# Softmax running sums: VectorE additions become accumulating transfers in GpSimd's queue

## The chip, the cores and the metric

The kernel runs on one core of a Trainium2 chip. The metric is the device time of one execution in microseconds (us). Beside it stands a profile: one execution recorded by the hardware profiler, with the busy time of each engine, what each waited for, and the transfers.

## The reference

The kernel computes a self-attention block on a feature map `x` of shape (16, 512, 32, 32) in float32: 16 images, 512 channels, 1024 positions, 4 heads of 128 channels each.

```python
xn = group_norm(x, 8 groups) * gamma + beta
q, k, v = split(einsum('oc,bchw->bohw', qkv_w, xn) + qkv_b, 3)   # to heads: (b, 4, 1024, 128)
attn = softmax(einsum('bhnd,bhmd->bhnm', q, k) * 128 ** -0.5)
out = einsum('bhnm,bhmd->bhnd', attn, v)                          # back to (b, 512, 32, 32)
return x + einsum('oc,bchw->bohw', proj_w, out) + proj_b
```

## The kernel before

The work is a sequence of **steps**, one for each image `b`, head `h` and block `j` of 128 keys: 16 x 4 x 8 = 512 steps. Keys lie on the 128 partitions and the 1024 queries along the row. In step `s`:

- `scores(s, half)` (L844 on): TensorE multiplies the key block by 512 queries (L846, tile `s` in PSUM), and ScalarE writes the exponentials into `p` (L852). A `p` tile is 128 x 1024, 512 KB; there are three of them.
- The softmax's denominators are the sums of the exponentials over all keys. VectorE first adds the eight blocks element by element into the tile `tot`: at block 1 it writes `tot` as the sum of blocks 0 and 1 (L858), and at blocks 2 to 7 it adds `p` to `tot` (L860). There is one `tot` tile.
- `weighted_sum(s - 1, half)` (L942): TensorE multiplies the values by the step before's `p`, adding over the eight blocks in the PSUM tile `po`. At the last block ScalarE copies `po` to the tile `o` (L949).

At block 1 of the next head `denominators` (L864 on) finishes the head before: VectorE transposes `tot` in 32 x 32 blocks (L869), reduces it (L871), adds the four partial results, transposes and takes the reciprocal (L879). Two transfers from ScalarE's queue spread it over the partitions (L891, L896, tile `rinv`), and at block 4 VectorE multiplies `o` by it (`divide`, L952). The very last head has its own ending, `last_division`, which lets TensorE do the sums over partitions.

Between the steps' products TensorE does the projections in 256- and 512-wide products by Strassen's scheme on two levels, spread over the heads by `plan_head`: queries and keys of the second head pair in head 0 (tiles `qk_*`), the output projection of the image before in head 1 (`pp_*`), queries and keys of the next image in head 2, its values in head 3 (`v_*`). For each product VectorE makes sums of the right-hand blocks (L574, tiles `qk_t`, `pp_t`), and VectorE and ScalarE empty the accumulators (L630, L486, L628). The weights' sums are kept in DRAM and come group by group by SP's queue into two buffers (`w<-kept`, L408).

GpSimd's queue carries transfers in the kernel before: `x` of the next image (L235), sums of the right-hand blocks that are used again (`kept_t`, L580), the values on their way through DRAM for a change of layout (`vd<-vu`, L779, then four `v<-vd`, L784, which wait for it), the residual `y<-in_x` (L813) and the result (L830). The tiles `vt`, `vu` and most `y` share four buffers with the tag "y".

A scheduler orders each engine's instructions when the kernel is built, by priority and by the order in which the program states them; each engine then runs its list in that order and waits on semaphores. `tc.high_priority(URGENT)` raises a priority, and `tc.issue_after(ins)` keeps the instructions inside it behind the named one. The dictionary `added` holds the additions to `tot` for that purpose: the group norm's small steps for the next image (`stats_group`), the first right-hand sums of the next image (`make_sum`), and `divide` are placed after the addition of a given block.

Of the kernel before, what the change touches and what calls it, by code (L numbers as in the profile page):

```python
# [13 lines left out]
ALU = mybir.AluOpType  # L14
# [13 lines left out]
URGENT = 40  # L28
# [158 lines left out]
def fast_path(ctx, tc, x, sources, out, consts, flag, dims):  # L187
# [6 lines left out]
    nc = tc.nc  # L194
    B, C, N, NCC, NH2, NB, GC, SCALE = dims
# [76 lines left out]
    def stats_group(b):  # L272


        g = []

        def part(n, first, last):
            if not g:
                g.extend(norm.group_steps(mvs[b]))
            with tc.issue_after(added[b - 1, 1, n].ins), tc.high_priority(URGENT):  # L280
                for step in g[first:last]:
                    step()

        def scale():
            n = 4 if b > 1 else 3
            part(n, 9, 10)
            with tc.issue_after(added[b - 1, 1, n].ins), tc.high_priority(URGENT):
                mu, sc = norm.result
                sh = norm.shift(mu, sc)
            for c in range(NCC):  # L290
                scaled[b, c] = sc, sh, c

        return [lambda: part(2, 0, 6), lambda: part(3, 6, 9), scale]
# [174 lines left out]
    def run(units):  # L468
        for u in units:
            u()  # L470
# [52 lines left out]
    def two_levels(name, site, b, blocks, finish, sums="make", homes="BBBB", prepare=None):  # L523
# [18 lines left out]
        def sum_tile(g, m):  # L542
            k = int(m[1]) - 1
            tag = f"in_{m}" if homes[g] == "B" else f"ot{2 + k // 2}{k % 2}"
            if homes[g] == "C":
                if k % 2 == 0:
                    pairs[g] = ppool.tile([P, N], F32, tag="p", name=f"{name}_{g}_{m}")
                t = pairs[g][:, ts(k % 2, HALF)]
            else:
                t = tpool.tile([P, HALF], F32, tag=tag, name=f"{name}_{g}_{m}")  # L550
            haves[g][m] = t.rearrange("p (i q) -> p i q", q=Q)
            return haves[g][m][:, : len(OUTER[g])]

        def inner_block(g, i, m):
            if m[0] == "t":
                return haves[g][m][:, i, :]
            outer = blocks()[FACTORS[OUTER[g][i]][1]]
            return outer[int(m[1]) - 1][:, ts(int(m[2]) - 1, Q)]

        def make_sum(g, m):  # L560
            n = len(OUTER[g])
            to = sum_tile(g, m)
            a, c = {
                "t1": ("b12", "b11"), "t2": ("b22", "t1"), "t3": ("t2", "b11"),
                "t4": ("b21", "t2"),
            }[m]
            with ExitStack() as order:
                if sums == "keep" and g == 0 and m in ("t1", "t2"):


                    order.enter_context(tc.issue_after(added[b - 1, 1, NB - 1].ins))
                    order.enter_context(tc.high_priority(URGENT))
                for i in range(n):
                    nc.vector.tensor_sub(  # L574
                        to[:, i, :], inner_block(g, i, a), inner_block(g, i, c)
                    )
            if sums == "keep":
                t = dpool.tile([P, n, Q], F32, tag=f"{m}_{g}", bufs=1, name=f"kept_{m}_{g}")
                inner_kept[b, g, m] = t
                nc.gpsimd.dma_start(t, to)  # L580
# [125 lines left out]
    def qk_groups(b, pair):  # L706

        def finish(which, r, a, c):
            of, half = int(which[1]) - 1, int(which[2]) - 1
            st, h = (qs, ks)[of], 2 * pair + r  # L710
            if (b, h) not in st:
                st[b, h] = qkpool.tile([P, N], F32, tag=f"qk{of}", name=f"qk{of}_{b}_{h}")
            i = of * HEADS + h
            nc.vector.scalar_tensor_tensor(  # L714
                st[b, h][:, ts(half, HALF)], a, qkb_sb[:, i : i + 1], c, ALU.add, ALU.add
            )

        return two_levels(
            f"qk_{b}_{pair}", pair, b, lambda: xb[b], finish,
            "make" if pair or b == 0 else "keep",  # L720
            "ABBB" if pair else "ABAB" if b > 0 else "BCBC",
        )
# [33 lines left out]
    def v_groups(b):  # L756
        rows = {}


        def finish(which, h, a, c):  # L760
            pair, half = int(which[1]) - 1, int(which[2]) - 1
            if (b, pair) not in vs:
                vs[b, pair] = vpool.tile(
                    [P, NH2, 2, P, NB // NH2], F32, tag="v", name=f"v_{b}_{pair}"
                )
            n = P // BLK
            t = ypool.tile([P, HALF], F32, tag="y", name=f"vt_{b}_{pair}_{h}_{half}")
            nc.vector.tensor_add(t, a, c)

            u = ypool.tile([P, HALF], F32, tag="y", name=f"vu_{b}_{pair}_{h}_{half}")  # L770
            nc.vector.transpose(  # L771
                u.rearrange("p (q i j) -> p j q i", q=n, i=BLK),
                t.rearrange("p (j q i) -> p j q i", q=n, i=BLK),
            )
            if h == 0:
                rows[which] = dpool.tile(
                    [2 * P, HALF], F32, tag="v", name=f"vd_{b}_{pair}_{half}"
                )
            nc.gpsimd.dma_start(rows[which][ts(h, P), :], u)  # L779
            if h == 0:  # L780
                return

            for q in range(n):
                nc.gpsimd.dma_start(  # L784
                    vs[b, pair][ts(q, BLK), half].rearrange(
                        "m h (k i) j -> m (h k) (i j)", k=n
                    ),
                    rows[which].rearrange("(k m) (q e) -> q m k e", m=BLK, q=n)[q],
                )

        return two_levels(f"v_{b}", "v", b, lambda: xb[b], finish, "load", "ABAB")
# [43 lines left out]
    ps, tot, po, rinv, last_eviction = {}, {}, {}, {}, {}  # L835
    inverse, rows_of, added, exps = {}, {}, {}, {}
    steps = B * HEADS * NB

    def where(s):
        bh, j = divmod(s, NB)  # L840
        return (*divmod(bh, HEADS), j)

    def scores(s, half):
        b, h, j = where(s)  # L844
        sc = ps_s.tile([P, HALF], F32, tag="s", name=f"s_{s}_{half}")
        nc.tensor.matmul(  # L846
            sc, ks[b, h][:, ts(j, P)], qs[b, h][:, ts(half, HALF)], start=True, stop=True
        )
        if half == 0:
            ps[s] = ppool.tile([P, N], F32, tag="p", name=f"p_{s}")  # L850
        with tc.high_priority(URGENT):
            exps[s] = nc.scalar.activation(ps[s][:, ts(half, HALF)], sc, AF.Exp, scale=SCALE)  # L852
        i = ts(half, HALF) if s == steps - 1 else ds(0, N)
        if j == 0 or (half == 0 and s < steps - 1):
            return
        if j == 1:
            tot[b, h] = lpool.tile([P, N], F32, tag="tot", name=f"tot_{b}_{h}")
            nc.vector.tensor_add(tot[b, h], ps[s - 1], ps[s])  # L858
        else:
            added[b, h, j] = nc.vector.tensor_add(  # L860
                tot[b, h][:, i], tot[b, h][:, i], ps[s][:, i]
            )

    def denominators(b, h):  # L864

# [85 lines left out]
    def divide(b, h):  # L951
        nc.vector.tensor_mul(os_[b, h], os_[b, h], rinv.pop((b, h)))  # L952
# [288 lines left out]
    for s in range(steps + 1):  # L1241
        units = []
        if s < steps:
            b, h, j = where(s)
            if j == 0:
                plan = plan_head(b, h)
            units = plan[j]
            if j == NB - 1 and h == 2 and b + 1 < B:
                next_v.append(v_groups(b + 1))
                next_qk.append(qk_groups(b + 1, 1))  # L1250
                units.append(ahead[f"v_{b + 1}"])
        if NB < s < steps and s % NB == 1:
            denominators(*where(s - 2)[:2])
        for half in range(NH2):
            if s < steps:
                scores(s, half)
                if j in (1, 2) and half == 1 and s > NB:
                    with tc.issue_after(exps[s].ins):
                        spread_inverse(*where(s - NB)[:2], j - 1)
                if half == 1 and j == 4 and s > NB:  # L1260

                    with tc.issue_after(added[b, h, 4].ins):
                        divide(*where(s - NB)[:2])
            if s > 0:
                weighted_sum(s - 1, half)
            n = (len(units) + 1) // 2
            run(units[half * n : (half + 1) * n])
        if s > 0:
            del ps[s - 1]
# [134 lines left out]
```

## Time and profile before

| what | value |
|---|---|
| time, median of 2 runs | 3171.86 us (3171.75 to 3171.98) |
| the profiled execution's span | 3170.7 us |
| granted TensorE clock | 1.000 |
| TensorE busy | 3159.9 us (100%) |
| VectorE busy | 2633.6 us (83%) |
| ScalarE busy | 1439.7 us (45%) |
| GpSimd busy | 517.7 us (16%) |
| additions L860 | 385, 1218 ns each, 469.0 us in all |
| transfers | 524.32 MB, mean 165 GB/s |

The span runs from the first to the last instruction that the profiler recorded; the time of a run also holds what lies around it. A line of the cost table names the program line, the engine, the operation, the written and the read tiles, the shapes and the count, then the busy time, the mean of one, and the idle time ahead of them with what ended most of it. A line of the transfers names the issuing queue, the count, the size of each and the median time from issue to landing. The timeline's columns are start, duration, engine, line, operation and, in brackets, the idle time ahead of it and what ended it.

### The profile page before, as it was taken

How to read it: one execution, taken by the hardware profiler on the slowest of the kernel's cores; microseconds unless marked ns; L12 is line 12 of the kernel's file. 1: busy time of each engine (PE TensorE's matmuls, PEld its weight loads, DVE VectorE, ACT ScalarE, POOL GpSimd, SP SyncE). 2: the span in 40 equal slices, each digit the busy share in tenths (PEclk: the TensorE clock that was granted, in tenths of full speed). 3: DMA queues.
4: the chain of work that ended last, by engine and by line, in shares of the span. 5: the costliest groups of instructions: out<-in, count | busy, mean ns of one | idle time of the engine just before them, and what ended most of it. 6: DMA issues, size and time to landing. Idle time of an engine off the chain costs nothing.

```text
span 3170.7 us, 34267 instructions
## 1 busy us (share of the span) xinstructions
PE 3159.9 (100%) x10524; PEld 2190.7 (69%) x10524; DVE 2633.6 (83%) x4639; ACT 1439.7 (45%) x2712; POOL 517.7 (16%) x898
## 2 busy tenths in 40 slices
PE   9999999999999999999999999999999999999999
PEld 7566676677766676777767767677676776766764
DVE  9878879788897888878788787987879978788784
ACT  3535435354353543545435453453534545344342
POOL 0011221111211112211122111222012221122200
PEclk9999999999999999999999999999999999999999
DMA  5554554555545455454554545555455564555531
GB/s 177 185 190 154 188 172 154 171 153 192 171 164 162 153 185 175 167 167 145 191 172 162 171 145 187 171 172 172 144 175 169 176 189 134 174 162 186 179 116 41
DMA packets 210333, 524.32 MB, mean 165 GB/s; under 512 B 32096, under 2 KB 65376, under 8 KB 210144
## 3 DMA queue, kind: packets, MB, share of 16 engines
q1 hardware_dynamic: 132896, 282.12, 28.8%
q0 software_dynamic: 64000, 204.54, 19.2%
q10 hardware_dynamic: 13248, 35.39, 3.5%
q8 instruction: 87, 1.43, 0.2%
q14 instruction: 102, 0.84, 0.1%
HBM read 388.77 MB, written 133.17 MB: 165 GB/s over the span
## 4 chain that ended last, share of the span: by engine, by line
PE 96%; DVE 3%; DMA 0%; issue 0%; POOL 0%; SPq 0%; ACT 0%; DVEq 0%; POOLq 0%
PE po L942 27%; PE s L846 27%; PE qk_x L606 12%; PE qk_y L606 9%; PE pp_x L606 6%; PE v_x L606 6%; PE pp_y L606 4%; PE v_y L606 4%; PE lx L1031 0%; DVE qk_t L574 0%; PE ly L1031 0%; PE warm L1153 0%; DVE tot L860 0%; DVE qk L714 0%; DVE qk_r L630 0%
## 5 line engine op out<-in xcount | busy, mean ns | idle before, releaser
L942 PE MATMUL po<-p,v 128*128 128x512 f32 x2048 | 1049.5, 594 | 0.7 <-ACT p L852 0.7
L846 PE MATMUL s<-qk,qk 128*128 128x512 f32 x2048 | 1047.4, 593 | 0.3 <-DVE qk L714 0.3
L852 ACT ACTIVATE p<-s 128x512 f32<-128x512 f32 x1024 | 610.9, 597 | 961.0 <-PE s L846 957.2
L942 PEld LDWEIGHTS po<-p,v 128*128 128x128 f32 x2048 | 603.6, 302 | 322.7 <-issue 214.5
L860 DVE TENSOR_TENSOR tot<-tot,p 128x1024 f32<-128x1024 f32 x385 | 469.0, 1218 | 158.4 <-ACT p L852 156.3
L846 PEld LDWEIGHTS s<-qk,qk 128*128 128x128 f32 x2048 | 387.7, 190 | 88.6 <-issue 29.9
L606 PEld LDWEIGHTS qk_x<-qk_t,w 128*128 128x128 f32 x1344 | 251.8, 190 | 166.1 <-issue 75.3
L606 PE MATMUL qk_x<-qk_t,w 128*128 128x256 f32 x1344 | 356.3, 382 | 0.1
L486 ACT COPY qk_u<-qk_x 128x512 f32<-128x512 f32 (+1 forms) x256 | 136.3, 533 | 229.2 <-PE qk_x L606 229.2
L779 POOL DMA_DIRECT2D vd<-vu x120 | 66.7, 557 | 899.8 <-DVE vu L771 897.9
L630 DVE TENSOR_TENSOR qk_r<-qk_y,qk_u 128x512 f32<-128x512 f32 (+1 forms) x256 | 157.7, 616 | 34.7 <-ACT qk_u L486 21.6
L580 POOL DMA_DIRECT2D kept_t<-qk_t x240 | 129.4, 540 | 278.4 <-DVE qk_t L574 211.9
L606 PEld LDWEIGHTS pp_x<-pp_t,w_proj 128*128 128x128 f32 x630 | 117.2, 190 | 74.7 <-issue 32.3
L784 POOL DMA_DIRECT2D v<-vd x240 | 140.6, 593 | 167.1 <-DMA vd<-vu 70.3
L630 DVE TENSOR_TENSOR v_r<-v_y,v_u 128x512 f32<-128x512 f32 (+1 forms) x120 | 76.0, 633 | 110.6 <-ACT v_u L486 80.3
L606 PE MATMUL pp_x<-pp_t,w_proj 128*128 128x256 f32 x630 | 167.8, 383 | 0.0
L606 PE MATMUL v_x<-v_t,w_v 128*128 128x256 f32 x630 | 166.6, 381 | 0.0
L830 POOL DMA_DIRECT2D out_y<-y x120 | 66.0, 550 | 604.2 <-DVE y L829 602.4
L606 PEld LDWEIGHTS v_x<-v_t,w_v 128*128 128x128 f32 x630 | 118.4, 190 | 55.3 <-issue 19.1
L606 PE MATMUL qk_y<-x,w 128*128 128x256 f32 x512 | 142.1, 379 | 0.0
L714 DVE SCALAR_TENSOR_TENSOR qk<-qk_r,qkb_sb,qk_r 128x512 f32<-128x512 f32 x192 | 137.5, 743 | 1.6
L486 ACT COPY v_u<-v_x 128x512 f32<-128x512 f32 (+1 forms) x124 | 66.3, 535 | 157.1 <-PE v_x L606 130.3
(217 smaller groups left out, 4487.2 us busy)
## 6 DMA issues: line engine op xcount, KB each, us to landing
w<-kept SPq DMA_DIRECT2D x90, 512.0 KB, 3.7
kept_t<-qk_t POOLq DMA_DIRECT2D x180, 256.0 KB, 3.3
v_t<-kept_t SPq DMA_DIRECT2D x180, 256.0 KB, 2.9
w<-kept SPq DMA_DIRECT2D x90, 384.0 KB, 3.4
rinv<-row ACTq DMA_DIRECT2D x63, 512.0 KB, 4.9
x<-in_x POOLq DMA_DIRECT2D x60, 512.0 KB, 4.6
vd<-vu POOLq DMA_DIRECT2D x120, 256.0 KB, 3.1
v<-vd POOLq DMA_DIRECT2D x240, 128.0 KB, 4.2
```

The lines of the kernel that those rows point to most:

```text
L486: nc.scalar.copy(t[n][:, :width], t["x"][:, :width])
L580: nc.gpsimd.dma_start(t, to)
L606: nc.tensor.matmul(acc[:, ts(i, Q)], have["w"][t][:, i, slot, :], inner(i, bn), start=(first and i == 0), stop=True, skip_group_check=True,)
L630: nc.vector.tensor_add(dst, view(a), view(c))
L714: nc.vector.scalar_tensor_tensor(st[b, h][:, ts(half, HALF)], a, qkb_sb[:, i : i + 1], c, ALU.add, ALU.add)
L779: nc.gpsimd.dma_start(rows[which][ts(h, P), :], u)
L784: nc.gpsimd.dma_start(vs[b, pair][ts(q, BLK), half].rearrange("m h (k i) j -> m (h k) (i j)", k=n), rows[which].rearrange("(k m) (q e) -> ...
L830: nc.gpsimd.dma_start(out[b, ts(o, P), ts(half, HALF)], t)
L846: nc.tensor.matmul(sc, ks[b, h][:, ts(j, P)], qs[b, h][:, ts(half, HALF)], start=True, stop=True)
L852: exps[s] = nc.scalar.activation(ps[s][:, ts(half, HALF)], sc, AF.Exp, scale=SCALE)
L860: added[b, h, j] = nc.vector.tensor_add(tot[b, h][:, i], tot[b, h][:, i], ps[s][:, i])
L942: nc.tensor.matmul(po[b, h][:, i], v_block(b, h, j), ps[s][:, i], start=(j == 0), stop=(j == NB - 1),)
```

## The change

From block 2 of each head on, the addition of `p` to `tot` is no longer an instruction of VectorE but a transfer in GpSimd's queue whose destination is `tot` and which adds to what is there (`accum_op=ALU.add`). Block 1's addition, which writes `tot` first, stays on VectorE, and so do all additions of the last head of the last image (`s >= steps - NB`). Each transfer reads a whole `p` tile, 512 KB, once both halves of its exponentials are written, and needs the transfer before it to have landed in `tot`; `p` is free again when its transfer has read it and the weighted sum has used it.

Since a transfer isn't an instruction of VectorE, `added` now holds, for these blocks, the last instruction stated so far for VectorE (`last_on_vector`); the places that order work behind `added` are otherwise the same.

```diff
+    def last_on_vector():
+
+        return next(
+            i for i in reversed(nc.cur_bb.bb.instructions) if i.engine == mybir.EngineType.DVE
+        )
...
         if j == 1:
             tot[b, h] = lpool.tile([P, N], F32, tag="tot", name=f"tot_{b}_{h}")
             nc.vector.tensor_add(tot[b, h], ps[s - 1], ps[s])
-        else:
+        elif s >= steps - NB:
             added[b, h, j] = nc.vector.tensor_add(
                 tot[b, h][:, i], tot[b, h][:, i], ps[s][:, i]
-            )
+            ).ins
+        else:
+            nc.gpsimd.dma_start(tot[b, h], ps[s], accum_op=ALU.add)
+            added[b, h, j] = last_on_vector()
...
-            with tc.issue_after(added[b - 1, 1, n].ins), tc.high_priority(URGENT):
+            with tc.issue_after(added[b - 1, 1, n]), tc.high_priority(URGENT):
```

The last pair of lines stands for four places that read `added` (two in `stats_group`, one in `make_sum`, one ahead of `divide`): they lose `.ins`, since `added` now holds the instruction itself.

More of the change, by code (lines that the diff above doesn't have):

```diff
@@ L286, in scale @@
             part(n, 9, 10)
-            with tc.issue_after(added[b - 1, 1, n].ins), tc.high_priority(URGENT):
+            with tc.issue_after(added[b - 1, 1, n]), tc.high_priority(URGENT):
                 mu, sc = norm.result
@@ L568, in make_sum @@
                 if sums == "keep" and g == 0 and m in ("t1", "t2"):
-                    order.enter_context(tc.issue_after(added[b - 1, 1, NB - 1].ins))
+                    order.enter_context(tc.issue_after(added[b - 1, 1, NB - 1]))
                     order.enter_context(tc.high_priority(URGENT))
@@ L1260, in fast_path @@
                 if half == 1 and j == 4 and s > NB:
-                    with tc.issue_after(added[b, h, 4].ins):
+                    with tc.issue_after(added[b, h, 4]):
                         divide(*where(s - NB)[:2])
```

## The prediction

> **What bounds the kernel now.** I read the page's engine line and chain first, then the group of the edited line, then four neighbouring heads as windows, and last the transfers and the waits.
>
> ```profile
> PE 3159.9 (100%) x10524; PEld 2190.7 (69%) x10524; DVE 2633.6 (83%) x4639; ACT 1439.7 (45%) x2712; POOL 517.7 (16%) x898
> PE 96%; DVE 3%; DMA 0%; issue 0%; POOL 0%; SPq 0%; ACT 0%; DVEq 0%; POOLq 0%
> L860 DVE TENSOR_TENSOR tot<-tot,p 128x1024 f32<-128x1024 f32 x385 | 469.0, 1218 | 158.4 <-ACT p L852 156.3
> ```
>
> TensorE is busy all the time, and 96% of the chain that ended last is TensorE. The edited line L860 is VectorE work and isn't in that chain by name. The windows (image 8, one head each; columns are the stretch, its length, then busy time and count of PE, PEld, DVE, ACT, POOL, the granted clock, the DMA share and GB/s) ask whether "busy" hides slack:
>
> ```profile
> 1612.00:1661.00 49.00, 49.00 (x164) 34.51 (x163) 43.48 (x73) 19.05 (x35) 13.55 (x24) 1.00 0.57 176
> 1661.00:1710.00 49.00, 49.00 (x166) 34.11 (x166) 42.09 (x84) 33.60 (x70) 6.18 (x9) 1.00 0.41 137
> 1710.00:1759.00 49.00, 49.00 (x164) 34.47 (x164) 44.31 (x79) 19.05 (x34) 9.69 (x18) 1.00 0.61 207
> 1759.00:1808.00 49.00, 49.00 (x164) 34.43 (x163) 34.36 (x54) 19.21 (x35) 4.55 (x8) 1.00 0.50 152
> ```
>
> A head's 164 matmuls are 64 of 512 columns (s and po, 8 blocks x 2 halves x 2 products x 2 passes) and 100 of 256. Back to back, the timeline spaces the former 0.43 us apart and the latter 0.216 us (eight in 1.73 us on the chain): 64 x 0.43 + 100 x 0.216 = 49.1 us. That is the whole 49.0 us. So a head has no slack on TensorE that a freer VectorE could win. What can be won lies at the two ends and is at most 3170.7 - 3159.9 = 10.8 us by the busy time. The profiled span, 3170.7 us, is 1.2 us under the median of the runs, 3171.86; I add to the latter.
>
> **What is removed.** 63 heads x 6 blocks = 378 of the 385 adds; the last head's 7 stay. 378 x 1.218 = 460 us of VectorE, 7.3 us a head. By the paragraph above this buys nothing on the path: I take 0, bounds 0 to -10.8 us. VectorE falls to some 2170 us, 69%.
>
> **What is added.** 378 transfers of 512 KB in GpSimd's queue, each reading p and the running sum and writing the sum. Each also needs the sum that the one before left, so within a head they form a chain of six. Issue: POOL rows show 0.54 us for a transfer, so 378 x 0.54 = 204 us, and POOL goes from 517.7 to some 720 us, 23%: no bound. The traffic:
>
> ```profile
> q0 software_dynamic: 64000, 204.54, 19.2%
> ```
>
> 378 x 0.524 = 198 MB more in that queue is 18.6% of the sixteen engines if it moves like the copies there, and 37% if each byte costs two. With today's queues (28.8 + 19.2 + 3.5 = 51.5%) the mean is 70 to 89%. Weights have two buffers and land in under 4 us against some 12 us per group, so I cost their delay at nothing; if that cover goes, TensorE waits at each group's first product.
>
> **The price that decides: P**, the time from "p and the previous sum are there" to "the sum has landed". No accumulating transfer is in this trace. The nearest rows (KB each, median us from issue to landing):
>
> ```profile
> w<-kept SPq DMA_DIRECT2D x90, 512.0 KB, 3.7
> kept_t<-qk_t POOLq DMA_DIRECT2D x180, 256.0 KB, 3.3
> x<-in_x POOLq DMA_DIRECT2D x60, 512.0 KB, 4.6
> kept_t<-qk_t POOLq DMA_DIRECT2D x60, 128.0 KB, 2.4
> w<-kept SPq DMA_DIRECT2D x30, 192.0 KB, 2.3
> ```
>
> The landing counts from the issue's start: a vd transfer issued at 1595.81 released its reader at 1599.11, 3.30 us. Low end: a plain 512 KB load, 3.7 us. High end: kept_t grows 0.9 us per 128 KB, so 1.5 us fixed and 3.6 us of data at 512 KB; with the data paid twice, 8.7 us. Between: the w rows grow 1.4 us over 320 KB, so 2.24 us of data and 1.46 us fixed; paid twice, 5.9 us. I take P = 6.0, since the second read must pass through the same engines but 512 KB of one partition row each is the shape of the w row.
>
> The Trainium skill, "Collectives: The Full Stack", section "The bandwidth ceiling: the fold count and why AG ≠ RS ≠ AR", says an add in a transfer is slow not for the arithmetic but because "the add needs **two source reads**", which halves its rate; that speaks for paying the data twice, and no row here can show it. The skill's "DMA: Bandwidth & Descriptors", section "Anatomy of one DMA — SWDGE (gpsimd) path", gives 2.0 us plus bytes at 436 GB/s; with 2 x 524 KB that is an estimate of 4.4 us on idle engines, by which the change would be free (the first rival).
>
> **Where P meets the path.** The denominators start with a transpose of the finished sum on VectorE (L869), an in-order engine. Image 8, head 2, is the tightest; second-half exponentials of blocks 2 to 7, then the transpose:
>
> ```profile
> 1726.75 0.60 ACT L852 ACTIVATE p<-s 128x512 f32<-128x512 f32 x1 [2.60 <-PE s L846]
> 1733.64 0.60 ACT L852 ACTIVATE p<-s 128x512 f32<-128x512 f32 x1 [0.27 <-PE s L846]
> 1739.66 0.60 ACT L852 ACTIVATE p<-s 128x512 f32<-128x512 f32 x1 [2.79 <-PE s L846]
> 1745.68 0.60 ACT L852 ACTIVATE p<-s 128x512 f32<-128x512 f32 x1 [0.27 <-PE s L846]
> 1751.81 0.60 ACT L852 ACTIVATE p<-s 128x512 f32<-128x512 f32 x1 [0.92 <-PE s L846]
> 1756.53 0.60 ACT L852 ACTIVATE p<-s 128x512 f32<-128x512 f32 x1 [0.48 <-PE s L846]
> ```
> ```profile
> 1759.30 1.23 DVE L869 STREAM_TRANSPOSE tt<-tot 128x1024 f32<-128x1024 f32 x1
> ```
>
> With P = 6.0: p of block 2 is there at 1727.35 and its sum at 1733.35; block 3 has p at 1734.24, sum 1740.24; then 1746.26, 1752.28, 1758.41 (block 6), and block 7 waits for block 6: 1764.41. The transpose stood at 1759.30, so it is 5.1 us late. The same walk gives 1.8, 0, 5.1 and 4.1 us for heads 0 to 3 of this image, whose transposes now start 5.4, 9.0, 2.2 and 4.4 us after the last exponential. Queued behind it on VectorE are the sums that TensorE multiplies next (qk_t, pp_t) and the additions that empty its accumulators; the timeline around an L869 has these ready 1.2 us before TensorE uses them (qk_t done 1621.92, product 1623.16), and VectorE's idle gaps behind give a little back: I take 1.5. So a delay d reaches TensorE as about d - 1.5: 0.3 + 0 + 3.6 + 2.6 = 6.5 us an image. A scheduler that now places the transpose later softens this, waits in GpSimd's queue (next) sharpen it; I leave both out of the sum. 6.5 x 63/4 = **102 us**, so 3171.9 + 102, about 3275 us.
>
> **The rest of the wait's cover.** p has three buffers: block s+3's first exponential needs the transfer of block s landed. From p's end to that exponential is 15.8 us for block 2 of this head and 10.7 us for block 5 of head 3, the shortest I see in this image; 6 us plus a carry of under 2 fits, so cost nothing up to P about 8. If that cover goes, ScalarE stops and TensorE with it. GpSimd's queue is in order: a transfer waiting for its sum holds what is behind it (kept_t, vd, v, x, y, out_y), and they hold it:
>
> ```profile
> POOL v L784 <- DMA vd<-vu: 70.3, 33, 4.3
> ```
>
> kept_t and x are used some 10 us or more later and cost nothing. vd frees VectorE's four "y" buffers, which is the third rival.
>
> **The rivals.** (1) *Hidden anyway, not slower.* With P at 5 the same walk gives 0, 0, 3.1 and 1.2 us late, 1.6 us an image after the 1.5 us slack: 25 us at most, and nothing if the scheduler moves L869 by 2 us. Time 3180. For it: the 3.7 us row, and 7.3 us of freed VectorE per head to catch up with. Against: the second read on engines already 52% busy. It decides from P under about 5.3.
> (2) *The chain sets the pace.* At P = 8.5 a head takes 6 x 8.5 = 51 us plus transpose 1.2, first add 1.2 and some 2 us of VectorE work between, 55.4 against 48.8: +6.6 x 63 = 416 us, 3588. It takes over from P about 7.4. At 7 the transposes are 6.8, 3.7, 10.0 and 7.7 late; halved for the carry that a stall gives back, +170 to +210, about 3370. For it: the 8.7 us bound and engines at up to 89%. Against: the w row.
> (3) *GpSimd's queue blocks VectorE.* 8 vd transfers an image each wait half a P, 3 us; if half of that reaches VectorE's vt/vu buffers, 12 us an image, x 15 = 180 us, 3350. For it: the transpose L771 already waits on a vd transfer once here (0.57 us at 1612.49). Against: two of four buffers are usually free, and head 3 has VectorE least loaded (34 us of 49).
> (4) *Faster.* Bound 10.8 us, 3161.
>
> **How the numbers follow.** Forecast, transposes late (3210 to 3400): 0.36; hidden 0.31; chain 0.21; queue 0.10; visibly faster 0.02. The likeliest gives 3275. The range takes in the hidden case's upper part and the chain near its figure: 3174 to 3570. A measurement of this kernel tells about 2% from no change, 63 us: below 3108 is possible in no case worked out, 0.02 for the unseen; within 2% is the hidden case and the weakest tenth of the forecast's, 0.33; slower 0.65.
>
> **What would show it.** Right: the rows for tot<-p in the transfers near 6 us to land; L869 with idle time ended by a DMA, 2 to 6 us in heads 0, 2 and 3 and none in head 1; TensorE's busy time as now and its idle near 100 us, put down to VectorE's sums; VectorE near 2170 us. Wrong: landings under 5 us and L869 unwaited (hidden), exponentials that wait for a DMA (p's buffers, the chain at pace), or idle ahead of L771 ended by vd<-vu (queue).

## The result and the profile after

The changed kernel takes 3466.26 us (two runs, 3457.66 and 3474.87) against 3171.86: **9.25% longer**, ratio 1.0925, interval 1.0859 to 1.0991. The profiled execution's span is 3455.8 us, 285.1 more than before. First the page: engines, then the groups of the transfer (L870) and of the transpose that reads the finished sum (L878, formerly L869).

```profile
PE 3261.7 (94%) x10524; PEld 2215.2 (64%) x10524; DVE 2237.1 (65%) x4261; ACT 1437.5 (42%) x2712; POOL 847.1 (25%) x1276
L870 POOL DMA_DIRECT2D tot<-p x378 | 334.5, 885 | 1839.8 <-ACT p L858 592.4
L878 DVE STREAM_TRANSPOSE tt<-tot 128x1024 f32<-128x1024 f32 x63 | 78.4, 1245 | 372.1 <-DMA tot<-p 372.1
```

VectorE's busy time fell by 396 us, where 460 were expected. The durations of its instructions, added one by one, fell by 458; busy time counts records that overlap once, and 62 us less of them overlap now. TensorE, with the same 10524 products, lost time twice: its idle time went from 10.8 to 194.1 us (+183), and its busy time from 3159.9 to 3261.7 us (+102). The transpose had no such wait before; now it stands 372 us behind transfers. The queue and the landings:

```profile
q0 software_dynamic: 118432, 402.75, 49.4%
tot<-p POOLq DMA_DIRECT2D x378, 512.0 KB, 5.7
x<-in_x POOLq DMA_DIRECT2D x60, 512.0 KB, 8.4
```

A transfer lands after 5.7 us (median). The queue's engine time grew from 19.2% of 3170.7 to 49.4% of 3455.8 us, by 1098 us for 198 MB more: 5.5 us a megabyte, against 3.0 for the queue's transfers before, 1.9 times. The factor agrees with the sentence of the Trainium skill quoted in the prediction ("Collectives: The Full Stack", the bandwidth ceiling), that such an add needs two source reads. The reads themselves stand in no view.

**Where in an image.** I measure a head from its first exponential to that of the next, mean over images 1 to 14:

| us | head 0 | head 1 | head 2 | head 3 | image |
|---|---|---|---|---|---|
| before | 48.8 | 49.5 | 48.7 | 48.8 | 195.8 |
| after | 49.1 | 57.3 | 51.3 | 55.2 | 212.9 |

14 x 17.1 = 239 us; image 0 is 21 us longer (201.2 against 180.4) and the first three heads of image 15 17 us (142.6 against 125.4). Together 277 of the 285 us; the other 8 lie behind the first exponential of the last head (70.2 us to the end against 62.5). Two stalls, in heads 1 and 3, make 14 of the 17 us.

**Head 1 stops through ScalarE.** Timeline of image 8, where head 0's sum is awaited (the bracket is the idle time ahead and what ended it):

```profile
1812.66 1.25 DVE L878 STREAM_TRANSPOSE tt<-tot 128x1024 f32<-128x1024 f32 x1 [6.34 <-DMA tot<-p]
1813.83 0.65 DVE L630 TENSOR_TENSOR pp_r<-pp_y,pp_p 128x512 f32<-128x512 f32 x1
1814.40 1.20 DVE L880 TENSOR_REDUCE part<-tt 128x32 f32<-128x1024 f32 x1
1815.64 1.06 ACT L264 ACTIVATE junk<-x 128x1024 f32<-128x1024 f32 x1 [4.72 <-DVE part L880]
1816.69 0.57 ACT L958 COPY o<-po 128x512 f32<-128x512 f32 x1
1817.31 2.09 PE L951 MATMUL po<-p,v 128*128 128x512 f32 x2 [4.45 <-ACT o L958]
```

The next image's statistics (L264) write `junk`, which has the buffer of `tt`. So ScalarE waits until the late transpose and its reduction are through, the copy of `po` behind it is late, and TensorE waits 4.45 us for `po`'s bank. Before, the same pass also came right behind the reduction (done 1666.86), but waited only 0.14 us for it:

```profile
1663.77 0.68 DVE L630 TENSOR_TENSOR pp_r<-pp_y,pp_p 128x512 f32<-128x512 f32 x1
1664.37 1.23 DVE L869 STREAM_TRANSPOSE tt<-tot 128x1024 f32<-128x1024 f32 x1
1665.64 1.22 DVE L871 TENSOR_REDUCE part<-tt 128x32 f32<-128x1024 f32 x1
1666.89 1.06 ACT L264 ACTIVATE junk<-x 128x1024 f32<-128x1024 f32 x1
```

The buffer is what ends this wait, but it isn't alone. The pass also reads the next image's `x`, whose four loads now stand behind the sixth transfer in GpSimd's queue:

```profile
1807.57 2.48 POOL L235 DMA_DIRECT2D x<-in_x  x4
```

The first of them landed at 1813.9. Without the late transpose the pass could have begun 1.7 us earlier, and no more.

**Head 3 stops through VectorE.** Head 2's sum is awaited 13 us, and behind the transpose stand the additions that empty TensorE's accumulators:

```profile
1926.33 1.25 DVE L878 STREAM_TRANSPOSE tt<-tot 128x1024 f32<-128x1024 f32 x1 [13.11 <-DMA tot<-p]
1927.50 0.65 DVE L630 TENSOR_TENSOR v_r<-v_y,v_p 128x512 f32<-128x512 f32 x1
1928.21 0.70 PE L606 MATMUL v_y<-x,w_v 128*128 128x256 f32 x2 [3.32 <-DVE v_r L630]
1929.17 1.62 PE L852 MATMUL s<-qk,qk 128*128 128x512 f32 x2
```

**Each stall then costs again.** The two passes of po took 2.09 us and those of s 1.62 us, where 1.02 is usual. The windows behind the stalls (stretch, length, busy time and count of PE, PEld, DVE, ACT, POOL, granted clock, DMA share, GB/s):

```profile
1808.00:1812.00 4.00, 4.00 (x16) 2.86 (x15) 0.00 (x0) 1.42 (x3) 2.05 (x4) 1.00 0.93 137
1816.00:1820.00 4.00, 2.69 (x4) 1.54 (x5) 2.26 (x10) 3.97 (x10) 0.00 (x0) 0.60 0.67 272
1930.00:1934.00 4.00, 4.00 (x10) 2.23 (x10) 3.35 (x8) 1.08 (x2) 0.00 (x0) 0.64 0.01 1
```

The granted clock is 1.00 ahead of the first stall and 0.60 and 0.64 in the two windows behind; taken narrower (1816.9 to 1820.2 and 1929.5 to 1932.8) it is 0.50. The trace has 35 such stretches at 0.5, nearly all 3.4 or 6.8 us long. Over the span the clock is 0.974 (1.000 before), and 2.6% of 3456 us is 90 of the 102 us of added busy time. In the mean over images 1 to 14 TensorE idles 4.7 us in head 1 and 3.5 us in head 3, and the low clock costs 2.6 and 1.8 us more. The Trainium skill, "TensorE: Matmul & The Clock Gate", Part 1, says that the clock falls to half after an idle window of about 3.4 us and comes back after as much work; the factor and the 3.4 us agree. The length of the wait doesn't: a single wait of 2.02 us (from 1452.89) was followed by 3.4 us at 0.50 too. Of the 13 waits between 2.0 and 2.8 us in this trace 7 were, of the 27 from 3.3 us up all. The measurement decides: here a wait of 2 us can already cost.

**Why the sum is so late.** Image 8, head 2, four transfers in a row with nothing between them on GpSimd, and a window for each gap:

```profile
1896.15 0.86 POOL L870 DMA_DIRECT2D tot<-p  x1 [4.06 <-ACT qk_u L486]
1904.91 0.87 POOL L870 DMA_DIRECT2D tot<-p  x1 [7.90 <-ACT qk_p L486]
1910.31 0.85 POOL L870 DMA_DIRECT2D tot<-p  x1 [4.53 <-ACT qk_u L486]
1919.64 0.86 POOL L870 DMA_DIRECT2D tot<-p  x1 [8.48 <-issue]
```
```profile
1896.20:1904.90 8.70, 8.70 (x29) 5.88 (x28) 5.83 (x8) 3.34 (x6) 0.81 (x1) 1.00 0.98 273
1904.90:1910.30 5.40, 5.40 (x18) 3.52 (x17) 2.76 (x6) 1.96 (x5) 0.87 (x1) 1.00 0.82 190
1910.30:1919.60 9.30, 9.30 (x33) 6.68 (x32) 1.93 (x3) 4.38 (x8) 0.85 (x1) 1.00 0.92 237
```

Spacings 8.8, 5.4, 9.3 us. While the p's of blocks 5 to 7 had been there for 4 us and more (1900.0, 1906.1, 1910.9), each waited for the one before. In the two long gaps the DMA engines are busy 98% and 92%, in the short one 82%, with head 3's weights and right-hand sums in flight. Over images 1 to 14 the median spacing of transfers issued over 0.5 us behind their `p` is 5.6, 7.2, 7.2 and 7.8 us in heads 0 to 3. In head 3 some of these waited for other work in GpSimd's queue; those that waited for their predecessor alone are 7.5 us apart.

How late a sum is has to be read from the transpose's start, not from VectorE's wait, since VectorE now comes to the transpose at another time. In us after the head's last exponential, mean over images 1 to 14:

| us | head 0 | head 1 | head 2 | head 3 |
|---|---|---|---|---|
| transpose starts, before | 5.5 | 9.0 | 2.2 | 4.6 |
| VectorE is free for it, after | 2.4 | 6.1 | 2.4 | 17.3 |
| transpose starts, after | 8.8 | 9.6 | 14.7 | 17.9 |

So the transposes wait 6.4, 3.5, 12.3 and 0.6 us, but start 3.3, 0.6, 12.5 and 13.3 us later than before. The edit moved the transpose in VectorE's list too: head 0's stood behind the addition `pp_r` (L630) and now stands ahead of it, and head 3's stands behind such additions (`qk_r`) of the next head. No run separates this reordering from the transfers.

### The profile page after: what moved, and what is told of

Same layout as the page of the kernel before. It is cut to its first block, busy times and chain, and to the rows that moved or that the text cites. A ratio compares the mean times of both kernels' runs of the same rounds, so it can differ in the third digit from the quotient of the medians.

```text
span 3455.8 us, 34499 instructions
## 1 busy us (share of the span) xinstructions
PE 3261.7 (94%) x10524; PEld 2215.2 (64%) x10524; DVE 2237.1 (65%) x4261; ACT 1437.5 (42%) x2712; POOL 847.1 (25%) x1276
## 3 DMA queue, kind: packets, MB, share of 16 engines
q0 software_dynamic: 118432, 402.75, 49.4%
## 5 line engine op out<-in xcount | busy, mean ns | idle before, releaser
L951 PE MATMUL po<-p,v 128*128 128x512 f32 x2048 | 1072.8, 606 | 66.5 <-ACT o L958 65.8
L852 PE MATMUL s<-qk,qk 128*128 128x512 f32 x2048 | 1066.7, 603 | 13.7 <-ACT p L858 13.4
L870 POOL DMA_DIRECT2D tot<-p x378 | 334.5, 885 | 1839.8 <-ACT p L858 592.4
L878 DVE STREAM_TRANSPOSE tt<-tot 128x1024 f32<-128x1024 f32 x63 | 78.4, 1245 | 372.1 <-DMA tot<-p 372.1
L630 DVE TENSOR_TENSOR qk_r<-qk_y,qk_u 128x512 f32<-128x512 f32 (+1 forms) x256 | 158.1, 617 | 97.1 <-ACT qk_u L486 55.8
L580 POOL DMA_DIRECT2D kept_t<-qk_t x240 | 142.1, 627 | 188.3 <-DVE qk_t L574 159.0
L606 PE MATMUL pp_x<-pp_t,w_proj 128*128 128x256 f32 x630 | 183.0, 410 | 4.3 <-ACT pp_p L486 3.2
L630 DVE TENSOR_TENSOR qk_r<-qk_y,qk_p 128x512 f32<-128x512 f32 (+1 forms) x128 | 79.0, 617 | 131.4 <-PE qk_y L606 131.2
L771 DVE STREAM_TRANSPOSE vu<-vt 128x512 f32<-128x512 f32 x120 | 133.4, 1112 | 10.2 <-DMA vd<-vu 9.7
L606 PE MATMUL qk_y<-qk_t,w 128*128 128x256 f32 x448 | 121.9, 389 | 17.8 <-DVE qk_r L630 17.8
```

The lines of the kernel that those rows point to most:

```text
L606: nc.tensor.matmul(acc[:, ts(i, Q)], have["w"][t][:, i, slot, :], inner(i, bn), start=(first and i == 0), stop=True, skip_group_check=True,)
L630: nc.vector.tensor_add(dst, view(a), view(c))
L771: nc.vector.transpose(u.rearrange("p (q i j) -> p j q i", q=n, i=BLK), t.rearrange("p (j q i) -> p j q i", q=n, i=BLK),)
L852: nc.tensor.matmul(sc, ks[b, h][:, ts(j, P)], qs[b, h][:, ts(half, HALF)], start=True, stop=True)
L870: nc.gpsimd.dma_start(tot[b, h], ps[s], accum_op=ALU.add)
L878: nc.vector.transpose(tt.rearrange("p c m -> p (c m)"), t)
```

## The experiments

Theory A: the time is lost where the transpose waits for the end of the chain. Theory B: the transfers cost by themselves, by load on the DMA engines, by GpSimd's in-order queue or by holding p. Times stand against 3466 us for the changed kernel and 3172 before. Most are single runs: differences under some 20 us aren't read.

**Transfers to a tile that nobody reads.**

```diff
+            added[b, h, j] = nc.vector.tensor_add(
+                tot[b, h][:, i], tot[b, h][:, i], ps[s][:, i]
+            ).ins
+            if s < steps - NB:
+                if j == 2:
+                    sink[b, h] = dpool.tile([P, N], F32, tag="sink", bufs=1, name=f"sink_{b}_{h}")
+                    nc.gpsimd.dma_start(sink[b, h], ps[s])
+                else:
+                    nc.gpsimd.dma_start(sink[b, h], ps[s], accum_op=ALU.add)
```

> All sums are made on VectorE as before; beside them each p of blocks 2 to 7 also goes by a transfer in GpSimd's queue to a DRAM tile that nobody reads (block 2 a plain copy, blocks 3 to 7 accumulating). So the 378 transfers, their queue, their hold on p's three buffers and nearly their traffic are there, but no engine waits for the last one. Theory A (the time is lost where the transpose of the sum waits for the end of the chain): 3172 to 3210 us, TensorE's clock 1.00, no transpose waiting for a DMA. Theory B (the transfers cost by themselves: load on the DMA engines, GpSimd's queue, p's buffers): 3350 us or more.

Measured: 3325.9 us, clock 0.986. Neither. Heads 2 and 3 are back at 49.0 and 48.7 us: there A holds. Head 1 is still at 56.5, by another wait than A's, as the list of waits shows:

```profile
ACT junk L264 <- DMA x<-in_x: 92.2, 15, 9.0
```

The next image's x stands behind head 0's chain in GpSimd's queue (in the changed kernel all four are issued at 1807.6, behind the sixth transfer; before, they were out by 1660.9, 6 us ahead of the first pass). So B has a part: the queue makes x late, and the same instruction L264 stops ScalarE.

**The transpose reads another tile.**

```diff
-        nc.vector.transpose(tt.rearrange("p c m -> p (c m)"), t)
+        nc.vector.transpose(tt.rearrange("p c m -> p (c m)"), ps[(b * HEADS + h + 1) * NB])
```

> The changed kernel, but the transpose ahead of the denominators reads the p tile of the current head's block 0 instead of the sum; what is left out is that the denominators come from the sums. The whole chain of accumulating transfers stays, and the next head's first addition still waits for its end. Theory A: the waits of the transposes (372 us in all) are gone, 3180 to 3270 us; what is left comes from that first addition, some 5 to 10 us further back. Theory B: 3400 us or more, as changed.

Measured: 3269.8 us, clock 0.990, at the upper end of A. Heads 47.5, 53.8, 48.8 and 50.8 us: with the chain kept and only the transpose freed, head 3 loses 4.5 and head 2 2.5 of its excess. B's 3400 is out. Head 1 keeps 4.4 us over before, again through GpSimd's queue, as the list of waits shows (ScalarE's normalising of `x`, L109, and what it comes from):

```profile
ACT x L109 <- DVE sh L102: 61.4, 16, 5.1
DVE sc L76 <- POOL rstd L90: 50.3, 16, 4.5
```

GpSimd also computes a step of the next image's group norm (`rstd`). In image 8 its input was there at 1749.0, but it started at 1751.7, behind a residual load that waited for an earlier result to be out. Behind ScalarE's wait for it TensorE waits 2.29 us for a copy of `pp_x`.

**The statistics later on ScalarE.**

```diff
-                spread(plan, [lambda c=c: stats_chunk(b + 1, c) for c in range(NCC)], 2, 4)
+                spread(plan, [lambda c=c: late_stats(b + 1, c) for c in range(NCC)], 2, 4)
+    def late_stats(b, c):
+        with tc.issue_after(exps[max(exps)].ins):
+            stats_chunk(b, c)
```

> The changed kernel, with the next image's four statistics passes on ScalarE placed behind the exponentials of head 1's blocks 2 and 3 instead of as early as they fit. They write a tile that shares its buffer with the transposed sum. Theory A with this sharing as the way by which head 0's late sum stops ScalarE and TensorE in head 1 (57.3 us a head there against 49.5 before): head 1 falls to 50 to 52 us, 3460 falls by 80 to 110 to about 3350 to 3380 us. If VectorE's own wait stalls head 1 anyway, or theory B holds: within 30 us of 3460.

Measured: 3378.5 us, 88 less; head 1 falls from 57.3 to 51.5, head 3 stays (56.4). The transposes wait as long as before (361 us in all), so in head 1 it is ScalarE's early passes, not VectorE's wait, that reach TensorE. The move takes them out of the way of the late transpose and of the late x at once, so it doesn't divide the loss between these two.

**The same edit on the first experiment.**

> The run with all sums on VectorE and the transfers into a DRAM tile that nobody reads (3325.9 us), with the statistics on ScalarE behind the exponentials. There head 1 took 56.5 us because ScalarE waited for the next image's x, which stands behind head 0's transfers in GpSimd's queue. Theory A: head 1 falls to 50 to 52 us, 3325 falls by 65 to 95 us to 3230 to 3260. If load on the DMA engines slows that head: within 25 us of 3326.

Measured: 3249.8 us, 76 less; head 1 at 50.9. Heads are 50.5, 50.9, 48.8, 48.9, image 0 still 21 us too long. So with nobody waiting for the sum and ScalarE out of the way, the transfers still cost some 78 us. In head 0 the step from block 1's second exponential to block 2's takes 7.8 us instead of 6.0; ScalarE's exponentials wait 88 us in all for transfers to release p, which I take for the cause without having separated it.

**Three blocks instead of six.**

```diff
-        elif s >= steps - NB:
+        elif s >= steps - NB or j > 4:
```

> The changed kernel with transfers for blocks 2, 3 and 4 alone (189 of 378); blocks 5 to 7 are added on VectorE. Theory A: the chain ends two to three blocks ahead of the transpose, so 3175 to 3220 us, clock near 1.00. Theory B: half the transfers, half the loss, about 3315 us.

Measured: 3230.4 us, clock 0.998: between the two, nearer to A. The transposes no longer wait for a transfer at all, but VectorE's own addition of a later block does, 94 us (25 times).

**Half the width.**

```diff
+            lo, hi = ts(0, HALF), ts(1, HALF)
+            nc.gpsimd.dma_start(tot[b, h][:, lo], ps[s][:, lo], accum_op=ALU.add)
+            added[b, h, j] = nc.vector.tensor_add(tot[b, h][:, hi], tot[b, h][:, hi], ps[s][:, hi]).ins
```

> The changed kernel with the transfers on the first 512 of the 1024 columns (256 KB each); VectorE adds the other half. If the landing is mostly data paid twice, it falls from 5.7 to about 3.7 us and the transposes no longer wait: 3180 to 3220 us. If most of it is fixed or queueing (landing still above 5 us): 3300 us or more.

Measured: 3205.9 us, clock 0.999, and in the transfers:

```profile
tot<-p POOLq DMA_DIRECT2D x378, 256.0 KB, 3.7
```

As expected of data paid twice: 378 transfers, the same queue, but 3.7 us each. In heads 0 to 2 none waits for its predecessor any more (in head 3, where GpSimd's queue waits for vd, 31 of 70 are still issued late), and the image takes 197.1 us. The transposes wait 87 us instead of 372, not nothing. So the number of transfers doesn't decide. The run halves the chain's length and the traffic together and can't tell these two apart.

**Transpose and first addition a block later** (with the statistics later; the edit states `denominators` behind the first exponential of block 2, and the first addition, of blocks 0 and 1, at block 2).

```diff
-        if NB < s < steps and s % NB == 1:
-            denominators(*where(s - 2)[:2])
+                if half == 0 and j == 2 and s > NB:
+                    with tc.issue_after(exps[s].ins):
+                        denominators(*where(s - NB)[:2])
...
+        if j == 2:
+            tot[b, h] = lpool.tile([P, N], F32, tag="tot", name=f"tot_{b}_{h}")
+            nc.vector.tensor_add(tot[b, h], *pair)
```

> The changed kernel with all 378 transfers; the statistics on ScalarE behind the exponentials as in the run before, and the transpose of the sum, with the next head's first addition, moved from block 1 to block 2 of the next head, some 6 us later. Theory A (the loss of the inner images is these two waits on the late sum): heads 2 and 3 back to about 49 us, head 1 about 51, an image 198 to 201 us against 212.9; 3215 to 3250 us with what the first and the last image lose (21 and 17 us). If the transfers cost by themselves (theory B): 3330 us or more.

Measured: 3376.2 us, as with the statistics alone: a miss, and the reason is in the kernel, not in the theory. The transpose of head 2 still waits 13.0 us (mean): it started at 1885.3 in image 8, ahead of block 2's exponential that it was to follow. So `tc.issue_after` kept the order only in the scheduler's plan; on the chip VectorE comes to the transpose when its list does, and waits. The delay that I meant to give wasn't given, so this run decides nothing on head 3.

**The same, transfers in images 1 to 14 alone.**

> The run above, with the transfers in images 1 to 14 alone (336); images 0 and 15 add on VectorE. Theory A with the first image's short steps as the cause of its loss: another 25 to 38 us less than the run above, 3180 to 3215 us. If the first image's loss has another cause: as the run above.

Measured: 3335.2 us (four runs, 3325 to 3347), ratio 1.052 (1.0488 to 1.0552): 41 less than the run above, a little more than expected. The time itself misses 3180 to 3215, since the run above had missed. Image 0 falls from 205.4 to 182.2 us and the first three heads of image 15 from 142.9 to 132.3. That image 0 suffers for its short steps isn't shown. Its head 1 takes 33.3 us before, less than six landings, and 49.3 in the changed kernel, which is 16 of the image's 21 us. But there ScalarE's pass (L264) also waits 8.5 us for the reduction and TensorE 6.5 us behind it, the way that head 1 of the other images stops.

**Other transfers out of GpSimd's queue.** kept_t, vd and v go to SP's queue.

```diff
-                nc.gpsimd.dma_start(t, to)
+                nc.sync.dma_start(t, to)
...
-            nc.gpsimd.dma_start(rows[which][ts(h, P), :], u)
+            nc.sync.dma_start(rows[which][ts(h, P), :], u)
```

> The changed kernel with kept_t, vd and v issued from SP's queue instead of GpSimd's, so that in heads 2 and 3 GpSimd's queue holds little but the accumulating transfers. In the changed kernel the spacing of transfers that wait for the one before is 5.6 us (median) in head 0, 7.2 in head 2 and 7.8 in head 3. If GpSimd's in-order queue stretches the chain: both fall to about 5.7 us, the transposes' wait in head 3 (12 us each) falls to under 6, and the time to 3380 us or less. If the load on the DMA engines does: head 2 stays at 7 us or more and its transpose's wait stays above 10 us; head 3 alone may fall, since there the queue waits for vd; 3430 to 3480 us.

Measured: 3481.5 us, just above the load's range. Spacings in head 2 stay at 7.5 us and its transpose waits 10.6 us: there the queue's order doesn't stretch the chain, and load is what is left; no run took the load alone away. In head 3 the mean falls from 8.6 to 7.0 us and the sum lands 10.3 us after the last exponential instead of 17.8, so the queue did hold those back. That bought nothing: head 3 falls from 55.2 to 51.2 us, but head 0, where head 3's sum is awaited, rises from 49.1 to 53.8, and its transpose now waits 4.6 us instead of 0.6.

**Two blocks, images 1 to 14** (`elif j > 3 or not 0 < b < B - 1:`).

> Transfers for blocks 2 and 3 alone, in images 1 to 14 (112 of 378); VectorE makes the rest. The chain then ends four blocks ahead of the transpose and nothing is near it. It takes 136 us of additions from VectorE. If VectorE's time is worth nothing here, as the prediction had it: 3172 to 3190 us, not faster than before. If it is worth a tenth of what is taken away: 3155 to 3162 us.

Measured: 3210.5 us (four runs), ratio 1.012 (1.0103 to 1.0137): 38 us slower, outside of both ranges, though under the 2% that count as a clear change. VectorE is relieved by 127 us, and no gain shows. The expectation that nothing is near the chain's end was wrong, since the list of waits shows VectorE's next addition behind the second transfer:

```profile
DVE tot L866 <- DMA tot<-p: 40.4, 28, 4.2
```

That two transfers cost this much hides what the relief alone is worth; that it is nothing rests on TensorE's 49.0 busy us in a head of 49.0 before. No version tried beats the kernel before.

## Why the prediction went wrong

- **Bound, and the worth of VectorE's relief: right.** TensorE's products are the same, and no run with less VectorE work was faster (1.012 with 127 us less).
- **P: right at the median, wrong as one number.** 6.0 us were taken, 5.7 measured, and 3.7 for half the bytes against some 3.7 by the same split (1.46 + 2.24). But the walk used it for every transfer, while those of head 2 were spaced 7.2 us and up to 9.3. The share of the DMA engines had been worked out (70 to 89%; 78% measured over the queues) and then costed at nothing, and the waits in GpSimd's queue were left out of the sum. So the lateness of the sums was mis-sized: 1.8, 0, 5.1 and 4.1 us were walked, 3.3, 0.6, 12.5 and 13.3 measured, 29.7 us an image instead of 11.0. Head 2's is put down to the load, by elimination; head 3's is in the main the queue's (7.5 us less with vd, v and kept_t out of it).
- **"A delay d reaches TensorE as about d - 1.5", through VectorE: wrong, and the step that failed most.** Each head's late sum cost the head behind it 7.8, 2.5, 6.5 and 0.3 us, where the prediction had 0.3, 0, 3.6 and 2.6. Of the 10.6 us an image by which 6.5 fell short of 17.1, 7.5 are head 0's sum: it was 3.3 us late and cost 7.8. Its way is ScalarE's, where `junk` shares the buffer of `tt` and late x stands close behind. The code shows the sharing (tag "tt" in `stats_chunk`), and the prediction didn't look at who else uses the tiles behind the late one. Moving the statistics took 88 us off. In the other direction, head 3's sum was 13.3 us late and cost next to nothing, with its transpose placed later in VectorE's list, which the prediction named and left out. With the measured lateness the same rule would give 24.6 us an image, too much; the two errors partly cancel.
- **"kept_t and x are used some 10 us or more later and cost nothing": wrong for x.** With sums on VectorE, late x alone stopped ScalarE for 92 us. The group norm's step `rstd` in the same queue wasn't listed at all.
- **A stall counted once: wrong.** The slower clock behind the stalls is some 90 of the 285 us (TensorE's busy time grew by 102); neither the sum nor a rival had it, so a TensorE busy time "as now" was wrong.
- **Left out:** image 0 and image 15, 38 us more than before, where the prediction counted every image as image 8. Whether their shorter steps are the reason stays open.
- **p's buffers "cost nothing up to P about 8": not quite.** Exponentials waited 152 us for transfers; in head 0 of the changed kernel little of it arrives (49.1 against 48.8).
- **The rivals.** "Hidden" is out. "The chain sets the pace" didn't come about in the inner images (a head of 49 to 57 us against 6 x 5.7 = 34), but it came near in head 3, where the chain takes 48.0 us from the first issue to the last landing. "The queue blocks VectorE at vu" gave 9.7 us of waits for vd at L771 and is out; the queue did block, but at x and at `rstd`.

## What to carry over

A chain of transfers must be walked with the landing time under the load that the change itself makes, at the place where it ends, not with a median or a quiet one. How late its result is shows in the start of what reads it; the reader's wait also counts how early its engine arrived. When a result becomes late, list every instruction that waits for the buffers behind it, on all engines, since the loss can arrive through an engine that has nothing to do with the change. And where the bounding engine has no gap, relieving another buys nothing, while each stall of a few microseconds is paid again in clock.

## What the runs showed of the hardware

The issue of an accumulating transfer kept GpSimd 0.885 us against 0.54 for plain ones. Its landing was 5.7 us for 512 KB and 3.7 us for 256 KB, and it took 1.9 times the engine time per byte. The landing doesn't show this factor everywhere: into the DRAM tile of the first experiment plain copies of 512 KB landed in 6.3 us, accumulating ones in 6.4. TensorE's granted clock fell to 0.50 for 3.4 or 6.8 us after every wait of 3.3 us or more, and after 7 of 13 waits between 2.0 and 2.8 us.
